# A matrix product by 11 block products instead of 12, with a new order of the steps around it

## The chip, the core and the metric

The kernel runs on one core of one Trainium2 chip. The metric is device time in microseconds: before, 270.99 us, the median of three runs (270.95 to 271.12). The core has a matrix engine (TensorE, PE in the profile, with PEld for its weight loads), three engines for elementwise work (VectorE or DVE, ScalarE or ACT, GpSimd or POOL) and SyncE (SP), which issues the transfers. Each takes its instructions strictly in the order in which the kernel writes them here.

## What is computed

Cross-attention with 8 heads of width 256, a residual and a layer norm. x is 16 batches x 256 rows x 256; the context has 16 batches x 77 rows x 192. All is float32.

```
Q = (x @ Wq)   K = (c @ Wk)   V = (c @ Wv)          # split into 8 heads of 256
score = Q K^T / sqrt(256), masked                   # 16 x 8 x 256 x 77
ctx = softmax(score) V, heads side by side          # 16 x 256 x 2048
out = ctx @ Wo + x
result = (out - mean) * rsqrt(var + eps) * gamma + beta
```

## The kernel before

**Folded weights.** Per head, Wq Wk^T / 16 is formed once (256 x 192: its transpose lies in `gA`, context columns 0 to 127, and in `gB`, columns 128 to 191, two heads in two halves of the partitions), and Wv Wo once (`uA`, `uB`). The context lies transposed in `cA` (128 partitions) and `cB` (64, in both halves). Per batch and head then A = g c^T (256 x 77) takes the place of Q and K, and scores are x A. `prepare_a` (line 168) makes A for a group of four batches and a pair of heads: `part_A` contracts 128 context columns in tiles of 128x32, `part_B` the other 64 in tiles of 64x32, 308 columns (4 x 77) at a time, into four banks. ACT copies these out (`copy_out`, line 960). `prepare_vw` (line 218) makes the same for values, one batch at a time, also in two parts.

**Softmax.** For each tile t of 128 rows (two a batch): `scores` (TensorE), `shift` (line 312: mask and row minimum, DVE, from two banks), `exponential` (ACT, eight heads, one instruction and one read of the sum each), `weigh` (reciprocal on DVE, two products on POOL), `turn` (transposition on DVE).

**Values.** `seven` (line 437) multiplies the weights of a batch's two tiles by seven instead of eight block products; it needs sums of the weights (`sums`, POOL, four instructions) and differences of the values (`differences`, POOL, one). `add_seven` (line 478) adds the products to x: two additions on DVE from PSUM, five on POOL. **Norm.** `finish` (line 500) makes mean and variance of a row tile (DVE), `spread` (line 522) the reciprocal deviation (ACT), `normalise` (line 565) two DVE instructions and the store.

**Order.** The main loop (line 977) runs b from -1 to 14. Step b works on three batches: scores and softmax of b + 1, `seven(b)`, norm of b - 1. Where (b + 1) is even, the step is long: `work_of(b + 1)` and `work_of(b + 2)` prepare the values of the next two batches and two pairs of heads of A for the next group. In a long step TensorE does scores, then parts A of the first work, parts B of both, parts A of the second, then `seven`; in a short step scores, then `seven`. What a short step leaves of its norm is done on DVE in the next step, after `shift` (`behind`). From b = 13 on, steps differ and stay as they are. All TensorE results go through eight PSUM banks in rotation (`ps_mm`): a new result waits until the one eight before it has been read.

**Setup.** Before the loop the weights are folded, A of the first group is made, the context's last part is turned (`turn_rest`, `turn_rest_last`, lines 634 to 641, with copies on POOL), and the last 13 context rows of all batches are multiplied (`prepare_last`, `pr`, eight banks, copied out by ACT and DVE in turn).

Of the kernel before, what the change touches and what calls it, by code (L numbers as in the profile page):

```python
# [27 lines left out]
def kernel(  # L28
# [52 lines left out]
    gB = const.tile([P, NF, DI], F32, tag="gB", name="gB")  # L81

# [85 lines left out]
    def prepare_a(g, places, lo=0, hi=GB, rest_first=False):  # L168


        if 0 in places:
            a_of[g] = in_two("a", [P, 2, GB, H, S2], g)
        parts = [
            (2 * u + i, dc) for u in places for dc in range(2) for i in range(2)
        ]
        batches = slice(g * GB + lo, g * GB + hi)
        each = GB // (hi - lo)
        whole = [
            ps_mm.tile([P, each, hi - lo, S2], F32, tag="mm", name=f"pa_{g}_{h}_{dc}_{lo}")
            for h, dc in parts[: len(parts) // each]  # L180
        ]
        banks = [w[:, i] for i in range(each) for w in whole]
        opening, closing = range(len(whole)), range(len(parts) - len(whole), len(parts))

        def cols(dc, i):
            return slice((2 * i + dc) * BK, (2 * i + dc + 1) * BK)

        wide = 2 if len(places) == 1 and g == 0 else 1

        def part_A():  # L190
            for n, ((h, dc), o) in enumerate(zip(parts, banks)):
                for i in range(NM):
                    nc.tensor.matmul(  # L193
                        flat(o[i * BK : (i + 1) * BK]),
                        gA[:, h, cols(dc, i)],
                        flat(cA[:, batches, :]),
                        start=not rest_first and n in opening,
                        stop=rest_first and n in closing,
                    )

        def part_B():
            for j in range(0, len(parts), 2):
                for i in range(0, NM, wide):
                    for k, (h, dc) in enumerate(parts[j : j + 2]):
                        nc.tensor.matmul(  # L205
                            flat(banks[j + k][i * BK : (i + wide) * BK]),
                            gB[half(k), h // 2, dc * P + i * BK : dc * P + (i + wide) * BK],
                            flat(cB[half(k), batches, :]),
                            start=rest_first and j + k in opening,
                            stop=not rest_first and j + k in closing,  # L210
                        )

        def copies():
            return [(a_of[g][:, dc, lo:hi, h, :], o) for (h, dc), o in zip(parts, banks)]

        return part_A, part_B, copies

# [94 lines left out]
    def shift(t):  # L312
# [17 lines left out]
        s_of[t] = s, top  # L330

# [168 lines left out]
    def finish(t):  # L500
# [3 lines left out]
        y = x_of(t)[:, 0, :]  # L504
        bn = st.tile([P, 6], F32, tag="bn", name=f"bn_{t}")
        nc.vector.bn_stats(bn, y)
        if j == 0:
            mv_of[g] = st.tile([P, GT, 2], F32, tag="mv", name=f"mv_{g}", bufs=2)
# [13 lines left out]
    def spread(first, last):  # L522
# [4 lines left out]
        nc.scalar.activation(log[:, lo:hi], mv_of[g][:, lo:hi, 1], AF.Ln, bias=eps)  # L527
# [72 lines left out]
    with tc.tile_pool(name="wonce", bufs=1) as wp:  # L600
# [33 lines left out]
        def turn_rest():  # L634
            nc.vector.transpose(flat(cA)[:, rest], flat(cA)[:, rest])
            nc.gpsimd.tensor_copy(cRA, cA[:, :, KM:])

        def turn_rest_last():
            nc.vector.transpose(flat(cB)[LB:, rest], flat(cB)[LB:, rest])
            nc.gpsimd.tensor_copy(flat(cB)[:LB, rest], flat(cB)[LB:, rest])  # L640
            nc.gpsimd.tensor_copy(cRB, cB[:, :, KM:])
# [163 lines left out]
        def g_of(e):  # L805
# [6 lines left out]
            nc.scalar.mul(gA[:, e], pg, D ** -0.5)  # L812
# [15 lines left out]
        def g_of_pair(a):  # L828
# [12 lines left out]
            for e, o in enumerate(banks):  # L841
                nc.scalar.mul(gA[:, 2 * a + e], o, D ** -0.5)
# [42 lines left out]
        for a in range(1, NF):  # L885
# [7 lines left out]
            a_of_pairs(a, rest_first=True)  # L893
        load_x(0)
# [10 lines left out]
        for j in range(NF // 2):  # L905
# [13 lines left out]
            for e, pw in enumerate(  # L919
# [3 lines left out]
                for i in range(2):  # L923
                    for k in range(2):
# [3 lines left out]
                        )  # L928
        for t in range(QT):
# [4 lines left out]
        turn_rest_last()  # L934
        sum_of(uB)
        for t in range(QT):
            exponential(t)
            weigh(t)

# [10 lines left out]
    def work_of(b, rest_first=False):  # L950
        g, n = b // GB + 1, b % GB
        work = [prepare_vw(b, rest_first)]
        if g < NG - 1 or g == NG - 1 and n < NF // 2:
            work.append(prepare_a(g, (n,), rest_first=rest_first))
        elif b <= NS:
# [21 lines left out]
    for b in range(-1, B - 1):  # L977
# [3 lines left out]
        for t in new if b >= 0 else ():  # L981
            scores(t)
        for t in new if b >= 0 else ():
# [8 lines left out]
        for m in range(0, 2) if b < 0 else range(b + 2, min(b + 3, B // 2)):  # L992
            turn_last(m)
        alone = b + 1 >= B - GB // 2
        works = work_of(b + 1) if alone or n % 2 == 0 else []
        for part_A, _, _ in works:
# [21 lines left out]
        for i, t in enumerate(new if b >= 0 else ()):  # L1018
            exponential(t)
            if old:  # L1020
                finish(old[i])
            weigh(t)
        ahead = works and not alone
        if old and not ahead:
            spread(old[0], old[-1] + 1)
        if ahead:
            copy_out(works)
            if old:
                spread(old[0], old[-1] + 1)
# [3 lines left out]
            for part_A, _, _ in works:  # L1033
# [6 lines left out]
        if b < NS:  # L1040
            if now:
                seven(b)
            if old:
                invert(old[0], old[-1] + 1)
                normalise(old[0])
            for t in new:
                turn(t)
            if b < 0:
                for t in range(QT, GT, 2):
                    transpose_x(t)  # L1050
                bias_of(GB, B)
# [8 lines left out]
            if now:  # L1060
                add_seven(b)
# [56 lines left out]
```

## Time and profile before

| what | us |
|---|---|
| median of the runs | 270.99 |
| the profiled execution, its own time | 269.95 |
| span of that execution | 268.2 |
| TensorE busy | 262.5 |
| DVE / ACT / POOL busy | 185.9 / 157.6 / 173.2 |

The span runs from the first to the last instruction of the profile; the rest of the 269.95 us lies around it. Busy times add up every instruction of an engine. The chain that ended last is followed back from the last instruction to whatever released each one; its lines give start, duration and what ran. In a timeline, a bracket at a line's end gives the idle time before it and the engine that ended it.

### The profile page before, as it was taken

The numbers are of one execution on the slowest core, as the hardware profiler recorded it, in microseconds if no ns is written. First come the engines' busy times: TensorE is split into PE (matmuls) and PEld (weight loads), VectorE is DVE, ScalarE is ACT, GpSimd is POOL, SyncE is SP. The second block draws the span as 40 slices with busy tenths as digits, with TensorE's granted clock in tenths as the row PEclk, the third lists the DMA queues.
The fourth block names the chain that finished last, engine by engine and source line by source line (L and its number), as shares of the span: only waits on it lengthen the run. The fifth ranks groups of instructions, "written<-read, shape, count | busy, mean of one in ns | idle before, by whom it ended". The sixth has DMA issues, their size and how long they took to land.

```text
span 268.2 us, 14455 instructions
## 1 busy us (share of the span) xinstructions
PE 262.5 (98%) x6090; PEld 191.8 (72%) x6090; DVE 185.9 (69%) x808; ACT 157.6 (59%) x667; POOL 173.2 (65%) x240
## 2 busy tenths in 40 slices
PE   8999999999999999999999999999999999999992
PEld 8566578944984699459944995499669957985662
DVE  1555967493583868665886379647977887799785
ACT  3243336536857565955596468737775595636772
POOL 1042005728399739994799669965998799585452
PEclk9999999999999999999999999999999999999999
DMA  6989987901500130232012401340034010100112
GB/s 190 217 199 228 334 138 142 311 21 34 129 7 2 46 80 2 63 111 71 5 43 90 112 5 43 91 113 2 6 120 122 4 45 2 44 22 22 46 40 80
DMA packets 41696, 22.69 MB, mean 85 GB/s; under 512 B 24144, under 2 KB 40608, under 8 KB 41632
## 3 DMA queue, kind: packets, MB, share of 16 engines
q1 hardware_dynamic: 41248, 20.98, 30.1%
q0 software_dynamic: 384, 0.79, 1.3%
q8 instruction: 48, 0.79, 1.3%
q14 instruction: 16, 0.13, 0.2%
HBM read 17.57 MB, written 4.19 MB: 81 GB/s over the span
## 4 chain that ended last, share of the span: by engine, by line
PE 98%; DVE 1%; issue 0%; DVEq 0%
PE ps L303 25%; PE pa L193 13%; PE pv L227 11%; PE po L450 11%; PE pm L450 8%; PE pa L205 6%; PE pv L238 6%; PE po L383 4%; PE pu L773 3%; PE pr L263 2%; PE pgb L834 2%; PE pw L787 1%; PE idle L703 1%; PE pr L274 1%; PE phb L850 1%; PE po L399 1%
## 5 line engine op out<-in xcount | busy, mean ns | idle before, releaser
L340 ACT ACTIVATE s<-s,top 128x77 f32<-128x77 f32 x256 | 85.3, 346 | 44.2 <-DVE top L320 37.9
L303 PE MATMUL ps<-a,xT 128*32 128x154 f32 x2048 | 69.9, 294 | 0.0
L303 PEld LDWEIGHTS ps<-a,xT 128*32 128x32 f32 x2048 | 66.2, 110 | 1.2 <-issue 0.4
L361 POOL TENSOR_TENSOR p<-s,rden 128x512 f32<-128x512 f32 x64 | 47.5, 768 | 29.5 <-DVE rden L355 29.4
L320 DVE CUSTOM_DVE_ANT_0 s<-ps,bias 128x77 f32<-128x77 f32 x256 | 43.5, 232 | 14.3 <-PE ps L303 14.3
L340 ACT ACTIVATION_READ_ACCUMULATOR s<-s,top 128x1 f32 x224 | 42.0, 187 | 0.0
L193 PE MATMUL pa<-cA,gA 128*32 128x308 f32 (+1 forms) x576 | 36.6, 395 | 0.0
L193 PEld LDWEIGHTS pa<-cA,gA 128*32 128x32 f32 x576 | 18.3, 110 | 21.0 <-issue 7.0
L484 POOL TENSOR_TENSOR xg<-xg,m 128x256 f32<-128x256 f32 x39 | 28.7, 736 | 6.6 <-DVE xg L498 4.5
L577 DVE SCALAR_TENSOR_TENSOR xg<-xg,rstd,bet 128x256 f32<-128x256 f32 x27 | 22.9, 847 | 14.0 <-ACT rstd L528 12.6
L227 PE MATMUL pv<-uA,cA 128*32 128x512 f32 x256 | 30.6, 595 | 0.0
L371 DVE STREAM_TRANSPOSE pT<-p 128x640 f32<-128x640 f32 x32 | 25.5, 821 | 3.4 <-POOL p L361 3.3
L414 POOL TENSOR_TENSOR ts<-vw 128x768 f32<-128x768 f32 x13 | 24.0, 1848 | 5.9 <-ACT vw L963 5.9
L963 ACT COPY vw<-pv 128x512 f32<-128x512 f32 x32 | 17.8, 584 | 14.8 <-PE pv L227 8.3
L498 DVE TENSOR_TENSOR xg<-po,xg 128x256 f32<-128x256 f32 x31 | 11.5, 405 | 13.8 <-PE po L450 13.3
L320 DVE DVE_READ_ACCUMULATOR2_ANT top<- 128x1 f32 x256 | 20.8, 81 | 0.0
L205 PE MATMUL pa<-cB,gB 64*32 64x308 f32 (+2 forms) x512 | 20.4, 387 | 0.0
L963 ACT COPY a<-pa 128x308 f32<-128x308 f32 (+1 forms) x56 | 18.9, 395 | 1.9 <-PE pa L193 0.4
L205 PEld LDWEIGHTS pa<-cB,gB 64*32 64x32 f32 (+1 forms) x512 | 11.0, 110 | 11.4 <-issue 6.2
L548 DVE SCALAR_TENSOR_TENSOR xg<-xg,mv,gam 128x256 f32<-128x256 f32 x30 | 17.6, 588 | 0.1
L238 PE MATMUL pv<-uB,cB 64*32 64x512 f32 x256 | 17.3, 597 | 0.0
L227 PEld LDWEIGHTS pv<-uA,cA 128*32 128x32 f32 x256 | 7.5, 109 | 12.8 <-issue 9.9
(119 smaller groups left out, 404.1 us busy)
## 6 DMA issues: line engine op xcount, KB each, us to landing
xg<-in_x_dram SPq DMA_DIRECT2D x8, 512.0 KB, 4.4
xT<-in_x_dram SPq DMA_DIRECT2D x56, 64.0 KB, 2.6
out_dram<-xg SPq DMA_DIRECT2D x11, 256.0 KB, 2.2
wo<-in_L_xattn_Wo_dram SPq DMA_DIRECT2D x4, 512.0 KB, 7.8
wq_blk<-in_L_xattn_Wq_dram SPq DMA_DIRECT2D x12, 128.0 KB, 4.3
out_dram<-xg SPq DMA_DIRECT2D x10, 128.0 KB, 1.9
wk_blk<-in_L_xattn_Wk_dram SPq DMA_DIRECT2D x12, 96.0 KB, 3.6
wvT<-in_L_xattn_Wv_dram POOLq DMA_DIRECT2D x8, 96.0 KB, 6.6
```

What stands on the lines that cost most here:

```text
L193: nc.tensor.matmul(flat(o[i * BK : (i + 1) * BK]), gA[:, h, cols(dc, i)], flat(cA[:, batches, :]), start=not rest_first and n in opening, ...
L205: nc.tensor.matmul(flat(banks[j + k][i * BK : (i + wide) * BK]), gB[half(k), h // 2, dc * P + i * BK : dc * P + (i + wide) * BK], flat(cB[ ...
L227: nc.tensor.matmul(pv[k][i * BK : (i + 1) * BK], cA[:, b, k * BK : (k + 1) * BK], uA[:, parts, :, i], start=not rest_first, stop=rest_first,)
L238: nc.tensor.matmul(pv[k][i * BK : (i + 1) * BK], cB[half(k), b, k * BK : (k + 1) * BK], uB[half(k), parts, :, i], start=rest_first, stop=n ...
L303: nc.tensor.matmul(ps[m // 2][i * BK : (i + 1) * BK, m % 2 * 2 * S2 : (m % 2 + 1) * 2 * S2], xT_of[t // PT][:, j * NM + m, dc], flat(a_of[ ...
L320: nc.vector.tensor_tensor_reduce(s[:, h], ps[a][:, k * S2 : (k + 1) * S2], bias[:, b, :], scale=-1.0, scalar=FAR, op0=ALU.add, op1=ALU.min ...
L340: nc.scalar.activation(s[:, h], s[:, h], AF.Exp, bias=top[:, one], scale=-1.0, accum_out=den[:, one] if summed_by_act(t) else None,)
L361: nc.gpsimd.tensor_tensor(part, e_mh[:, :, :, keys], rden_mh.unsqueeze(3).to_broadcast(list(part.shape)), ALU.mult,)
L371: nc.vector.transpose(pT_of[t].rearrange("p n m q -> p m n q"), p.rearrange("p m (n k) -> p m n k", k=BK),)
L450: nc.tensor.matmul(out[i * BK : (i + 1) * BK], weight[:, i], moving, start=first and n == 0, stop=final and n == len(terms) - 1,)
L484: nc.gpsimd.tensor_tensor(to, to, what, ALU.add)
L963: nc.scalar.copy(dst, src)
```

## The change

1. Ten of the pairs of heads (groups 1 and 2, and the first two pairs of group 3) are made by `prepare_fast` instead of `prepare_a`. The 256 x 192 matrix of a head is cut into blocks of 64 context columns by 128 rows, the context into the first two and the last two batches of a group (154 columns each). That would be 12 block products; by sums and differences of blocks made beforehand (`gS`, `gC` of the weights, `cT`, `cD` of the context) it is 11, each in tiles of 64x64. One product a head is needed in two sums: ACT copies it out alone, its bank slice is used again, and four DVE additions (`put_together`) make A from two banks and that copy.
2. Steps b = -1 to 8 become `quick_step`: both value products' 128-row parts, then `seven`, then all 64-row work; `finish` after both exponentials; `turn`, `sums`, `add_seven`, then the differences, the norm and, last in a long step, `put_together`. From b = 9 on the loop keeps its old form.
3. For batches 0 to 9 `finish` makes mean and variance on ACT, by two activations with a running sum.
4. Copies of `turn_rest` and `turn_rest_last` go from POOL to ACT. `gA` is stored with its columns in another order.

```diff
+    def sums_of_g():
+        for parts, sums, e, own, other in parts_of_g():
+            nc.scalar.copy(sums[own, 0, e], parts[other, 1, e])
+            nc.scalar.copy(gC[own], gB[other, :, P:])
+        for parts, sums, e, own, other in parts_of_g():
+            s1, s2, s3 = (sums[own, n, e] for n in range(3))
+            add(s1, s1, parts[own, 1, e])
+            subtract(s2, s1, parts[own, 0, e])
+            subtract(s3, parts[own, 0, e], parts[own, 1, e])
...
+    def sums_of_c(lo, hi):
+        xs, ys = halves_of(cA, lo, hi)
+        t1, t2, t3, t4 = (cT[:, n, lo - 1 : hi - 1] for n in range(4))
+        subtract(t1, ys, xs)
+        for own, other in ((low, high), (high, low)):
+            nc.gpsimd.tensor_copy(t2[own], ys[other])
+        subtract(t3, t2, ys)
+        subtract(t2, t2, t1)
...
+    def prepare_fast(g, u):
...
+        def middle(e):
+            h, own = heads[e], (high, low)[e]
+            return [
+                ((mids[e], 2), from_g(own, h, 0), c_of(cA, own, xs)),
+                ((mids[e], 0), from_s(own, 0, h), t_of(own, 0)),
+                ((mids[e], 2), from_s(own, 1, h), t_of(own, 1)),
+                ((mids[e], 1), from_s(own, 2, h), t_of(own, 2)),
+                ((mids[e], 1), lambda i: gC[own, u, half(i)], c_of(cB, own, ys)),
+            ]
+        def outer(e):
...
+        def pairs():
+            o, m = outer(0), middle(1)
+            ones = o[:2] + m[:1] + o[2:] + m[1:]
+            o, m = outer(1), middle(0)
+            return list(zip(ones, m[:1] + o[:3] + m[1:] + o[3:]))
+        def products():
...
+                for i in range(2):
+                    for ((bank, n), weight, moving), (start, stop, _) in zip(pair, flags):
+                        nc.tensor.matmul(bank[half(i), n], weight(i), moving, start=start, stop=stop)
+                for ((bank, n), _, _), (_, _, one) in zip(pair, flags):
+                    if one:
+                        nc.scalar.copy(blocks[lone[id(bank)]][:, 0], by_batch(bank)[:, n])
+        def plus(out, *of):
+            nc.vector.tensor_tensor(out, *of, ALU.add)
+        def put_together(e):
+            mid, end, of = by_batch(mids[e]), by_batch(ends[e]), blocks[e]
+            plus(of[:, 3], mid[:, 2], of[:, 0])
+            plus(of[:, 1:3], mid[:, 0:2], of[:, 3:4].to_broadcast([P, 2, HB, S2]))
+            plus(of[:, 3], mid[:, 0], of[:, 2])
+            plus(of[:, 0:3], end, of[:, 0:3])
+        return products, put_together
...
+    def by_act(t):
+        return fast(t // QT)
+    def fast(b):
+        return b < B - GB - GB // 2
...
+        if by_act(t):
+            junk = st.tile([P, DI], F32, tag="junk", name=f"junk_{t}", bufs=1)
+            mean, var = (mv_of[g][:, j, n : n + 1] for n in range(2))
+            nc.scalar.activation(junk, y, AF.Identity, scale=1.0 / DI, accum_out=mean)
+            nc.scalar.activation(junk, y, AF.Square, bias=mean, scale=-1.0, accum_out=var)
+            return
...
-            nc.gpsimd.tensor_copy(flat(cB)[:LB, rest], flat(cB)[LB:, rest])
-            nc.gpsimd.tensor_copy(cRB, cB[:, :, KM:])
+            nc.scalar.copy(flat(cB)[:LB, rest], flat(cB)[LB:, rest])
+            nc.scalar.copy(cRB, cB[:, :, KM:])
...
+    def quick_step(b):
...
+        if b >= 0:
+            for t in new:
+                exponential(t)
+                weigh(t)
+        for t in old:
+            finish(t)
+        if old:
+            spread(old[0], old[-1] + 1)
+        fasts = []
+        if long:
+            works = work_of(b + 1) + work_of(b + 2)
+            for part_A, *_ in works:
+                part_A()
+        if now:
+            seven(b)
+        if long:
+            for _, part_B, _ in works:
+                part_B()
+            for k in range(2):
+                fasts.append(prepare_fast(g, n + k))
+                if k == 0:
+                    copy_out(works[:1])
+                fasts[k][0]()
+                if k == 0:
+                    copy_out(works[1:])
+        for t in new:
+            turn(t)
...
+        sums(b + 1)
+        if now:
+            add_seven(b)
+        if long:
+            for k in range(2):
+                differences(b + 1 + k)
...
+        if long:
+            if old:
+                normalise(old[0])
+            turn_x_and_normalise(g, n, old)
+            for _, put_together in fasts:
+                put_together(0)
+                put_together(1)
+        else:
+            if old:
+                behind.append(partial(normalise, old[0]))
+            behind.append(partial(turn_x_and_normalise, g, n, old))
+
+    ready = B - GB - GB // 2 - 1
+    for b in range(-1, ready):
+        quick_step(b)
+    for b in range(ready, B - 1):
```

More of the change, by code (lines that the diff above doesn't have):

```diff
@@ L893 @@
             a_of_pairs(a, rest_first=True)
+        gS = const.tile([P, 3, H, P], F32, tag="gS", name="gS")
+        sums_of_g()
         load_x(0)
@@ L952, in work_of @@
         work = [prepare_vw(b, rest_first)]
[L953 to L955 removed]
+        if b <= NS and not fast(b):
             part = (0, 2) if g < NG else (2, GB)
@@ L980 @@
         new = range((b + 1) * QT, (b + 2) * QT)
-        for t in new if b >= 0 else ():
+        g, n = (b + 1) // GB + 1, (b + 1) % GB
+        long = n % 2 == 0
+        if b >= 0:
+            for t in new:
+                scores(t)
+            for t in new:
+                shift(t)
+        while behind:
+            behind.pop(0)()
+        if long and g < NG:
+            load_x((g * GB + n) // 2)
+        for m in range(0, 2) if b < 0 else range(b + 2, min(b + 3, B // 2)):
+            turn_last(m)
@@ L991 @@
             load_x((g * GB + n) // 2)
-        for m in range(0, 2) if b < 0 else range(b + 2, min(b + 3, B // 2)):
-            turn_last(m)
         alone = b + 1 >= B - GB // 2
-        works = work_of(b + 1) if alone or n % 2 == 0 else []
-        for part_A, _, _ in works:
+        ahead = not alone and n % 2 == 0
+        works = work_of(b + 1) if alone or ahead else []
+        for part_A, *_ in works:
             part_A()
@@ L1017 @@
             break
-        for i, t in enumerate(new if b >= 0 else ()):
+        for i, t in enumerate(new):
             exponential(t)
-            if old:
-                finish(old[i])
+            finish(old[i])
             weigh(t)
-        ahead = works and not alone
-        if old and not ahead:
-            spread(old[0], old[-1] + 1)
         if ahead:
             copy_out(works)
-            if old:
-                spread(old[0], old[-1] + 1)
+        spread(old[0], old[-1] + 1)
+        if ahead:
             works = work_of(b + 2, rest_first=True)
@@ L1032 @@
                 part_B()
-            for part_A, _, _ in works:
+            for part_A, *_ in works:
                 part_A()
@@ L1040 @@
         if b < NS:
[L1041 to L1045, printed above, removed]
+            seven(b)
+            invert(old[0], old[-1] + 1)
+            normalise(old[0])
             for t in new:
                 turn(t)
[L1048 to L1051, printed above, removed]
             if alone or ahead:
```

125 lines of the change are left out of this document (114 added, 11 removed).

## The prediction

> **What bounds the kernel now.** I read the share of the chain that ended last first, then that chain in order of time, then the busy times of one period, then the queues of VectorE (DVE), ScalarE (ACT) and GpSimd (POOL) in order of time.
>
> ```profile
> PE 98%; DVE 1%; issue 0%; DVEq 0%
> ```
>
> ```profile
> 134.95 1.72 PE pv L227 x16
> 136.67 2.07 PE pa L193 x32
> 138.74 1.02 PE pv L238 x16
> 139.76 1.04 PE pa L205 x32
> 140.79 0.86 PE pv L238 x16
> ...
> 142.69 1.85 PE pv L227 x16
> ...
> 146.62 1.75 PE pm L450 x64
> ...
> 150.54 4.19 PE ps L303 x128
> ...
> 162.83 1.72 PE pv L227 x16
> ```
>
> ```profile
> 134.77:162.65 27.88, 27.88 (x713) 20.22 (x705) 19.10 (x96) 18.18 (x83) 22.53 (x31) 1.00 0.21 60
> ```
>
> The chain is TensorE nearly from end to end. Its pieces touch: two steps (one "long", with the preparation of two batches, one "short") take 162.83 - 134.95 = 27.88 us, without a gap and at a granted clock of 1.00. The preparation, 134.95 to 146.62, is 11.67 of it; scores and seven products are the other 16.21, 8.1 a step, of which scores are 4.19. In the same window DVE works 19.10 us, ACT 18.18, POOL 22.53 (the columns after PE and PEld). So only TensorE's queue counts now, and a gain there lasts until another engine's queue is as long. Busy sums don't tell when that is: an engine in order also waits. So I lay out the waits.
>
> **TensorE's gain.** One pair of heads costs 2.07 + 1.04 = 3.11 us now (L193 and L205). Afterwards it is 11 products x 2 heads x 2 column halves = 44 matmuls of 154 columns, four at a time in 64x64 tiles. The profile shows every matmul as two instructions, so 88, or 22 fours. The scores, also 154 columns, run 128 instructions in 4.19 us: 0.131 us a four, so 2.88 us. For the 64x64 form there are these rows (start, duration):
>
> ```profile
> 13.29 1.10 PE L850 MATMUL phb<-qT,kT_all 64*64 64x128 f32 x32
> 14.22 1.91 PE L834 MATMUL pgb<-qT,kT_all 64*64 64x256 f32 x32
> ```
>
> 32 instructions of 128 columns take 14.22 - 13.29 = 0.93 us, 0.116 a four; scaled to 154 columns that is 0.140, or 3.08 us. So a pair gains 0.03 to 0.23 us; I take 0.23, since the scores have the right width. `prepare_fast` runs in the long steps b = -1, 1, 3, 5, 7, twice each: 10 x 0.23 = 2.3 us. Putting the 64-row work in one block removes no change of tile shape: there is one entry to 64 rows now (1.02 against 0.86 for the same work, 0.16 us) and one return (1.85 against 1.72, 0.13). A change from 64x32 to 64x64 tiles is added; before has none. I bound it by 0 and 0.16 and take 0.1, 0.5 us in five steps. TensorE alone would then need 27.88 - 2 x 0.23 + 0.1 = 27.5 us a period and save 1.8 us in all. The Trainium skill, "TensorEngine Tiling (Array Packing)", Tiling Modes, Key Properties, says that changing the tiling mode, not just the tile, drains the engine; by it the added change costs like the other entry, 0.8 us in five steps, and the 0.16 above agrees.
>
> **What VectorE gets for it.** Before, ACT copied the four A banks out. Now ACT copies one slice a head, and `put_together` is four DVE additions a head: 154, 308, 154 and 462 columns, one operand in PSUM. The trace has the same operation at two sizes:
>
> ```profile
> L498 DVE TENSOR_TENSOR xg<-po,xg 128x256 f32<-128x256 f32 x31 | 11.5, 405 | 13.8 <-PE po L450 13.3
> ```
>
> ```profile
> L516 DVE TENSOR_TENSOR xg<-po,xg 128x128 f32<-128x128 f32 x2 | 0.6, 286 | 0.0
> ```
>
> The slope is (405 - 286)/128 = 0.93 ns a column, so 0.31, 0.45, 0.31 and 0.60 us. The first three each feed the next, and a dependent instruction starts 0.04 after the end of the one before (145.88 + 0.44 to 146.36, below); independent ones overlap by some 0.1 (two of 0.83 in 1.56, below). One head: 1.6 us (1.3 if all overlap, 1.8 if none does). A long step has four heads: **6.4 us** (5.2 to 7.2). It stands at the end of the long step, and the next step's `shift` is queued behind it on DVE. Taken off DVE are the row statistics, but these fill waits of DVE for ACT today, so I count nothing for them.
>
> So DVE's queue closes a loop over two steps. Its short leg, from the first `shift` instruction to the end of the product additions, is in these rows:
>
> ```profile
> 151.65 0.24 DVE L320 CUSTOM_DVE_ANT_0 s<-ps,bias 128x77 f32<-128x77 f32 x1 [0.29 <-PE ps L303]
> 157.62 0.20 DVE L355 RECIPROCAL rden<-den 128x8 f32<-128x8 f32 x1 [0.96 <-ACT s L340]
> 159.29 1.56 DVE L371 STREAM_TRANSPOSE pT<-p 128x640 f32<-128x640 f32 x2
> 160.77 0.71 DVE L498 TENSOR_TENSOR xg<-po,xg 128x256 f32<-128x256 f32 x2
> ```
>
> ```profile
> 157.90 1.69 POOL L361 TENSOR_TENSOR p<-s,rden 128x512 f32<-128x512 f32 x2 [0.29 <-DVE rden L355]
> ```
>
> The second tile's reciprocal comes 5.97 us after the first `shift`, with ACT's 16 exponentials in between without a pause. POOL's weighing ends at 159.59, the second tile's transposition takes half of 1.56, the additions 0.71: 7.94 + 0.78 + 0.71 = **9.4 us**, which no order in the diff shortens. Only then, on DVE's queue, can the long step's `shift` run:
>
> ```profile
> 133.55 0.22 DVE L320 CUSTOM_DVE_ANT_0 s<-ps,bias 128x77 f32<-128x77 f32 x1
> 136.08 0.57 DVE L548 SCALAR_TENSOR_TENSOR xg<-xg,mv,gam 128x256 f32<-128x256 f32 x1
> 137.45 0.70 DVE L293 STREAM_TRANSPOSE vr<-vr 128x512 f32<-128x512 f32 x1
> 144.69 1.26 DVE L165 STREAM_TRANSPOSE xT<-xT 128x512 f32<-128x512 f32 x2
> 145.88 0.44 DVE L548 SCALAR_TENSOR_TENSOR xg<-xg,mv,gam 128x256 f32<-128x256 f32 x1
> 146.36 0.84 DVE L577 SCALAR_TENSOR_TENSOR xg<-xg,rstd,bet 128x256 f32<-128x256 f32 x1
> ```
>
> ```profile
> 140.62 2.90 POOL L361 TENSOR_TENSOR p<-s,rden 128x512 f32<-128x512 f32 x4
> ```
>
> `shift` 2.53 (133.55 to 136.08); two normalisations left over from the short step, 1.35 each (136.08 to 137.45, 145.88 to 147.20); one `vr` transposition 0.63; two reciprocals 0.2; POOL's weighing 2.90; the second transposition 0.78; additions 0.71; a normalisation, two `xT` transpositions and a normalisation 1.35 + 2.51. Together 14.3 us, then 6.4 of `put_together`: 20.7. **The loop is 9.4 + 20.7 = 30.1 us**, against 27.5 for TensorE after the change and 27.88 before. In today's order the same sum without `put_together` is 23.7, and TensorE hides it. Now it is DVE that sets the pace, and TensorE's 0.4 us a period is gone. Where the lateness reaches it: the first part of the sum that `prepare_fast` makes for a head stands in a bank slice that is used again, so the sixth pair of products waits for ACT's copy of it after the first, five pairs of 0.26 us later; ahead of that copy stand on ACT the exponentials, whose `shift` was late, `finish`, `spread`, the copy of `m` and those of `pv`, which also free banks of the same products. Excess 30.1 - 27.88 = 2.2 us, four periods (b = 1 to 9): 8.8. DVE enters the first of them early, being idle in b = -1; I take off half a period's excess: **+7.7** (a loop of 28.9 or 30.9 by the bounds of `put_together`, reckoned the same way: +3.6 to +10.6).
>
> The Trainium skill, "GPSIMD Engine Reference", Specifications, says that POOL shares its SBUF interface with VectorE and that instructions with two SBUF inputs contend. L577, with two, shows 0.84 above; L498, with one operand in PSUM, took 0.71 for two while POOL was busy. If the page's rule reached PSUM operands too, and stretched the additions by, say, a half, the loop would grow by 3.2 us; the trace is against that.
>
> **The start.** The copies of `turn_rest_last` move from POOL to ACT, ahead of the exponentials of the first batch, which on ACT stand ahead of the copies of `pr`:
>
> ```profile
> 48.79 0.93 POOL L640 COPY cB<-cB 64x896 f32<-64x896 f32 x1 [3.49 <-DVE cB L639]
> 49.78 0.36 POOL L641 COPY cRB<-cB 128x208 f32<-128x208 f32 x1
> ```
>
> ```profile
> 54.06 1.80 ACT L133 COPY vr<-pr 128x416 f32<-128x416 f32 x4 [3.28 <-PE pr L274]
> ```
>
> At the same prices ACT is through both at about 50.1, and with 16 exponentials (5.5 us, as in the 5.97 above) at 55.6. The copies of `pr`, which free the banks of the first `pv`, begin 1.5 us later than 54.06, and TensorE with them; the smaller preparation of b = -1 gives 0.4 back: **+1.1 us** (0.5 to 1.6). ACT's copies for `sums_of_g` and POOL's sums lie in idle time before 40 us; the sums of C before step b = -1 leave POOL enough time until the products need them. No DMA is added; the two loads of `xT` go out together, later on SP, and are turned a long step later.
>
> **The handover at b = 9.** The first step of the old form has exponential, `finish`, exponential, `finish` on ACT, as `by_act` still holds for batches 8 and 9. `finish` waits for batch 8's last addition on POOL, and `quick_step(8)` puts `sums(9)` ahead of it. Between these rows POOL does just this work, additions and sums, without a pause:
>
> ```profile
> 133.87 0.99 POOL L484 TENSOR_TENSOR m<-m 128x128 f32<-128x128 f32 x2
> 137.20 0.92 POOL L431 TENSOR_TENSOR ss<-pT 128x256 f32<-128x256 f32 x1
> ```
>
> From 133.87 to 140.62 it is 6.75 us. The price of ACT's statistics isn't shown; the nearest rows:
>
> ```profile
> L561 ACT ACTIVATE xg<-xg,rstd 128x256 f32<-128x256 f32 x3 | 1.5, 510 | 0.3 <-DVE xg L548 0.2
> ```
>
> ```profile
> L340 ACT ACTIVATION_READ_ACCUMULATOR s<-s,top 128x1 f32 x224 | 42.0, 187 | 0.0
> ```
>
> Two activations and two reads: 1.4 us end to end, 1.0 with no read; I take 1.1. Let T be the end of the last transposition of step 8. The sum is complete at T + 6.75; then `finish` 1.1, eight exponentials 2.7, `finish` 1.1, two copies 1.1: the banks of `pv` come free at T + 12.8. In the steady loop T lies 9.4 - 0.7 = 8.7 after the short step's first `shift`, that 3.2 to 4.6 after its scores begin (half to three quarters of `put_together`), and the scores of b = 9 begin 8.1 after those: T is 3.8 to 5.2 after them. TensorE needs the banks here:
>
> ```profile
> 186.53 4.19 PE ps L303 x128
> ...
> 195.91 0.52 PE pa L205 x32
> ```
>
> 195.91 - 186.53 = 9.4 us after these scores begin, and gets them at 16.6 to 18.0: a stall of **8 us** (4.4 if the additions should be done when the first exponentials end).
>
> **Rivals.** (1) **TensorE keeps the pace, faster.** It needs the loop at most 27.5, 2.6 less than my sum: `put_together` at 3.8 instead of 6.4. With no hole at b = 9 either, 1.8 us are saved: 269.95 - 1.8 + 1.0 (to the median, below) = 269.2, faster, if the start is hidden too; with the start's 1.5 it is 270.7, no change. For it: every busy sum stays below the period. Against it: 3.8 us is less than the columns alone (1,078 x 4 x 0.93 ns = 4.0). (2) **The loop only**: `finish` doesn't hold ACT at b = 9; 269.95 + 1.1 + 7.7 + 1.0 = 279.8. (3) **The handover only**: loop about 27.9; 269.95 + 1.1 + 8 + 1.0 = 280. (4) The 64x64 products don't run four at a time: not below 3.11 a pair, no gain, and the same loop; it changes my time by nothing, since TensorE waits anyway.
>
> **How the numbers follow.** The profiled execution took 269.95 us for a span of 268.2; the median of the runs is 270.99, 1.0 more, which I add. Forecast 269.95 + 1.1 + 7.7 + 8 = 286.8, with 1.0 **287.8**. Low end: start 0.5, loop 3.6, handover 4.4, 279.5; rivals 2 and 3 at some 280; a little below them 277. High end: 1.6 + 10.6 + 8.6 and 2 us of lag left in the steps after b = 9: 293.8; I take 295. Chances: forecast 0.60, rivals 2 and 3 0.12 each, rival 1 0.16, of which 0.04 with the start's cost, which is no change; rival 4 sits inside the forecast. About 0.2% is what a measurement of this kernel can tell from no change. Faster 0.12, same 0.04, slower 0.84.
>
> **What would show it.** Right: period of two steps near 30 us between b = 3 and b = 9, TensorE idle at the `pf` products or scores with ACT or DVE as releaser, `shift` following directly on the last addition of `put_together`, a hole of several us on TensorE at `pa` L205 in b = 9. Wrong: a chain still 98% TensorE and a period of 27.5; additions shorter than 0.2 us.

## The result, and the profile after

| | before | after |
|---|---|---|
| median, us (lowest to highest) | 270.97 (270.86 to 271.12, 4 runs) | 286.16 (285.49 to 286.43, 4 runs) |
| profiled execution, us (span) | 269.95 (268.2) | 285.92 (283.8) |
| first scores of b = 1, us | 74.81 | 76.44 |
| first scores of b = 9, us | 186.34 | 196.82 |
| first scores of b = 10, us | 203.08 | 217.71 |

The kernel after is slower: ratio 1.0557, 95% interval 1.0536 to 1.0577. The forecast was 287.8.

The page of the kernel after: span, busy times, two of the rows of slices (busy share of TensorE and its granted clock, each digit the tenths of a fortieth of the span), and the shares of the chain that ended last.

```profile
span 283.8 us, 15133 instructions
PE 265.9 (94%) x6330; PEld 205.1 (72%) x6330; DVE 205.3 (72%) x848; ACT 172.7 (61%) x736; POOL 188.7 (66%) x262
...
PE   8999999899998999979998999799968999999992
...
PEclk9999999999999999979999999999999999999999
...
DVE 25%; POOL 16%; ACT 13%; PE 9%; issue 3%; DVEq 0%; POOLq 0%; ACTq 0%
```

TensorE's row on the page of the kernel before:

```profile
PE   8999999999999999999999999999999999999992
```

The chain that was 98% TensorE now goes round through DVE, POOL and ACT, TensorE's row has holes in the middle where it had none, and the granted clock one dip (a 7). No engine but TensorE, which now waits, is near full: DVE has 72%. Busy shares would not have told this; a queue of instructions in order, with its waits, is the bound.

The same by periods of two steps, from the scores of b = 1 to those of b = 9. The first number after the window is its length, then PE, PEld, DVE, ACT and POOL busy, and the granted clock.

```profile
76.44:105.64 29.20, 28.29 (x761) 22.87 (x757) 21.29 (x99) 17.06 (x81) 21.30 (x29) 1.00 0.19 45
105.64:137.79 32.15, 30.16 (x761) 24.40 (x755) 24.92 (x106) 22.06 (x105) 22.82 (x31) 0.95 0.23 59
137.79:166.58 28.79, 27.82 (x760) 22.64 (x756) 23.59 (x102) 18.67 (x85) 20.69 (x28) 1.00 0.17 51
166.58:196.82 30.24, 28.49 (x760) 22.72 (x756) 23.35 (x102) 20.36 (x95) 21.73 (x29) 1.00 0.21 56
```

Together 120.38 us, 30.1 a period, where before had 4 x 27.88 = 111.5. Now DVE in order of time over one period: `shift` of the long step, its norm and transpositions, the additions, `shift` of the short step.

```profile
142.27 0.22 DVE L485 CUSTOM_DVE_ANT_0 s<-ps,bias 128x77 f32<-128x77 f32 x1
...
148.44 0.22 DVE L526 RECIPROCAL rden<-den 128x8 f32<-128x8 f32 x2
150.08 0.84 DVE L542 STREAM_TRANSPOSE pT<-p 128x640 f32<-128x640 f32 x1 [1.43 <-POOL p L532]
151.42 0.84 DVE L542 STREAM_TRANSPOSE pT<-p 128x640 f32<-128x640 f32 x1 [0.49 <-POOL p L532]
152.19 0.72 DVE L669 TENSOR_TENSOR xg<-po,xg 128x256 f32<-128x256 f32 x2
...
156.49 7.28 DVE L372 TENSOR_TENSOR a<-pf,a 128x154 f32<-128x154 f32 x16
163.68 0.23 DVE L485 CUSTOM_DVE_ANT_0 s<-ps,bias 128x77 f32<-128x77 f32 x1
...
166.90 0.20 DVE L526 RECIPROCAL rden<-den 128x8 f32<-128x8 f32 x1 [0.61 <-ACT s L511]
169.63 0.20 DVE L526 RECIPROCAL rden<-den 128x8 f32<-128x8 f32 x1 [2.53 <-ACT s L511]
...
172.74 0.22 DVE L485 CUSTOM_DVE_ANT_0 s<-ps,bias 128x77 f32<-128x77 f32 x1
```

The 16 additions (L372) take 7.28 us, and the next step's `shift` (L485) starts at 163.68 directly on their end. From 142.27 to 163.68 the long leg is 21.4 us; the short leg, to 172.74, is 9.1. ACT stood idle for the whole length of the additions:

```profile
164.01 0.36 ACT L511 ACTIVATE s<-s,top 128x77 f32<-128x77 f32 x1 [7.26 <-DVE top L485]
```

Where TensorE paid for it, by its own waits (total, times, longest):

```profile
PE pm L621 <- ACT vw L1145: 3.4, 1, 3.4
PE pf L360 <- DVE xg L669: 3.1, 4, 1.0
PE pf L360 <- ACT m L646: 1.9, 3, 0.7
PE pv L392 <- ACT vr L142: 1.2, 1, 1.2
PE pv L392 <- ACT m L646: 0.6, 2, 0.3
```

The first row is b = 9 alone, the fourth is the start, the others are the loop. They add up to less than the loss, in part because the clock fell behind the longest of the loop's waits (last section), which took 1.7 us of TensorE's time; the rest isn't traced.

The 16.0 us between the two profiled executions divide, by the scores' starts in the table, into 1.6 at the start (76.44 - 74.81), 8.9 in the four periods (120.38 - 111.53) and 4.1 in the step b = 9 (20.89 us against 16.74); 1.3 is behind it, 0.4 of that outside the span.

### The profile page after: what moved, and what is told of

The parts are those of the page before. It is cut to its first block, busy times and chain, and to the rows that moved or that the text cites. A ratio compares the mean times of both kernels' runs of the same rounds, so it can differ in the third digit from the quotient of the medians.

```text
span 283.8 us, 15133 instructions
## 1 busy us (share of the span) xinstructions
PE 265.9 (94%) x6330; PEld 205.1 (72%) x6330; DVE 205.3 (72%) x848; ACT 172.7 (61%) x736; POOL 188.7 (66%) x262
## 4 chain that ended last, share of the span: by engine, by line
DVE 25%; POOL 16%; ACT 13%; PE 9%; issue 3%; DVEq 0%; POOLq 0%; ACTq 0%
ACT s L511 11%; POOL p L532 7%; PE pf L360 6%; DVE pT L542 5%; DVE s L485 4%; DVE a L372 4%; PE ps L468 4%; DVE xg L725 3%; POOL xg L655 3%; DVE xg L754 3%; DVE xg L669 2%; POOL ss L603 1%; POOL ss L604 1%; POOL ss L602 1%; POOL ss L605 1%
## 5 line engine op out<-in xcount | busy, mean ns | idle before, releaser
L532 POOL TENSOR_TENSOR p<-s,rden 128x512 f32<-128x512 f32 x64 | 45.2, 730 | 40.3 <-DVE rden L526 40.2
L485 DVE CUSTOM_DVE_ANT_0 s<-ps,bias 128x77 f32<-128x77 f32 x256 | 41.6, 230 | 0.0
L372 DVE TENSOR_TENSOR a<-pf,a 128x154 f32<-128x154 f32 x80 | 33.6, 436 | 2.8
L655 POOL TENSOR_TENSOR xg<-xg,m 128x256 f32<-128x256 f32 x39 | 29.7, 763 | 2.7 <-DVE xg L669 0.7
L526 DVE RECIPROCAL rden<-den 128x8 f32<-128x8 f32 x32 | 6.0, 193 | 32.0 <-ACT s L511 31.8
L754 DVE SCALAR_TENSOR_TENSOR xg<-xg,rstd,bet 128x256 f32<-128x256 f32 x27 | 18.7, 692 | 6.9 <-ACT rstd L705 5.2
L485 DVE DVE_READ_ACCUMULATOR2_ANT top<- 128x1 f32 x256 | 20.5, 80 | 0.0
L360 PE MATMUL pf<-cT,gS 64*64 64x154 f32 x240 | 18.8, 306 | 0.0
L360 PEld LDWEIGHTS pf<-cT,gS 64*64 64x64 f32 x240 | 17.0, 141 | 0.0
L602 POOL TENSOR_TENSOR ss<-pT 128x256 f32<-128x256 f32 x13 | 9.7, 745 | 10.7 <-DVE pT L542 10.7
L360 PE MATMUL pf<-cA,gA 64*64 64x154 f32 x160 | 11.6, 302 | 5.0 <-DVE xg L669 3.1
```

The source lines that it names most:

```text
L360: nc.tensor.matmul(bank[half(i), n], weight(i), moving, start=start, stop=stop,)
L372: nc.vector.tensor_tensor(out, *of, ALU.add)
L485: nc.vector.tensor_tensor_reduce(s[:, h], ps[a][:, k * S2 : (k + 1) * S2], bias[:, b, :], scale=-1.0, scalar=FAR, op0=ALU.add, op1=ALU.min ...
L532: nc.gpsimd.tensor_tensor(part, e_mh[:, :, :, keys], rden_mh.unsqueeze(3).to_broadcast(list(part.shape)), ALU.mult,)
L655: nc.gpsimd.tensor_tensor(to, to, what, ALU.add)
L754: nc.vector.scalar_tensor_tensor(y, y, rstd, bet, ALU.mult, ALU.add)
```

## Experiments

Theory: **DVE's loop** (short leg, long leg with the additions at its end) sets the period; the wait of b = 9 and the start are separate terms. Rivals: the new order or the 64x64 products themselves are slow, or the pace is set by ACT with its statistics. The ratio is to the kernel before, run on the same chip (270.1 to 270.4 us there).

| run | edit | us | ratio, 95% |
|---|---|---|---|
| e1 | additions of two heads behind the next `shift` | 282.00 | 1.0420 to 1.0451 |
| e2 | statistics on ACT for batches 0 to 7 only | 281.74 | 1.0400 to 1.0440 |
| e3 | new order, 12 products as before | 274.40 | 1.0141 to 1.0172 |
| e4 | statistics all on DVE | 282.28 | 1.0430 to 1.0476 |
| e5 | additions and norms into DVE's waits, e2's edit | 273.24 | 1.0089 to 1.0123 |
| e6 | the start's copies back on POOL | 285.62 | 1.0545 to 1.0594 |
| e7 | e5 and e6 | 274.46 | 1.0131 to 1.0178 |
| e8 | e5, but one head's additions put off | 273.04 | 1.0074 to 1.0107 |
| e9 | e8, start's copies on POOL, sums of C placed | 270.65 | 1.0001 to 1.0019 |
| e10 | e9, one POOL addition later | 270.78 | 1.0009 to 1.0030 |
| e11 | e9, one normalisation later | 270.03 | 0.9977 to 1.0001 |
| e12 | e11, sums of C spread | 269.74 | 0.9958 to 0.9986 |

**e3: which half of the change costs?** The 11 products and `put_together` are replaced by `prepare_a`, in the new order.

```diff
-                fasts.append(prepare_fast(g, n + k))
+                plain = prepare_a(g, (n + k,), rest_first=True)
...
-                fasts[k][0]()
+                plain[1]()
+                plain[0]()
...
-            for _, put_together in fasts:
-                put_together(0)
-                put_together(1)
```

> The quick steps keep their order, their statistics on ACT and all sums made beforehand, but A comes from the twelve products of before (parts B, then A, four banks, ACT copies them out) in the place of the eleven, so the 16 additions of a long step are gone from DVE. Theory (the additions make the loop too long): loop 30.3 - 7.2 = 23, TensorE paces at 27.9 a period as before; left are the start (1.6) and the hole at b = 9, at most 4: 272 to 276 us. Rival (the new order of the steps itself is what costs): 282 us or more.

274.40. Two of its periods:

```profile
96.80:124.98 28.18, 28.18 (x708) 20.02 (x704) 17.91 (x88) 22.77 (x99) 21.09 (x30) 1.00 0.21 60
124.98:153.16 28.18, 28.18 (x708) 20.02 (x704) 17.90 (x88) 22.77 (x99) 21.83 (x30) 1.00 0.22 60
```

TensorE is busy for the whole of each. ACT's 22.8 us of work don't slow it, and b = 9 has no hole (17.03 us against 16.74 before). The period is 0.3 us over before. That fits the tile shapes: here TensorE goes to 64-row tiles and back twice a period, once for each pair of heads, before only once, and there the change cost 0.16 us and the one back 0.13. So 286.16 - 274.40 = 11.8 us come with the 11 products and their additions: the loop and, through its lateness, the handover (20.89 us).

**e1: is it the place of the additions on DVE?**

```diff
-            for _, put_together in fasts:
-                put_together(0)
-                put_together(1)
+            for e in range(2):
+                fasts[0][1](e)
+            behind.extend(partial(fasts[1][1], e) for e in range(2))
```

> The additions of the second pair of heads (8 of the 16 of a long step) go behind the shift of the next step; nothing else is changed. Theory (DVE's in-order queue closes a loop of 30.3 us over two steps): 3.6 us leave the long leg and fall in the short step, where DVE waits 0.6 + 2.5 us for ACT's exponentials anyway, so the loop becomes about 27.5 and TensorE paces again: four periods x 2.8 = 11 us less, 275 us. Rival (TensorE waits for banks that the additions of products and the copy of m free, and the place of the additions doesn't matter): 286 us, within 1 us.

282.00, between the two. The direction was the loop's, the size not. DVE in the short step of e1:

```profile
158.54 0.23 DVE L485 CUSTOM_DVE_ANT_0 s<-ps,bias 128x77 f32<-128x77 f32 x1
...
162.01 3.61 DVE L372 TENSOR_TENSOR a<-pf,a 128x154 f32<-128x154 f32 x8
165.54 0.26 DVE L526 RECIPROCAL rden<-den 128x8 f32<-128x8 f32 x2
167.22 0.84 DVE L542 STREAM_TRANSPOSE pT<-p 128x640 f32<-128x640 f32 x1 [1.43 <-POOL p L532]
```

The eight additions stand in front of both reciprocals. In the kernel after, the first of them comes 3.2 us after the first `shift` (166.90 - 163.68); here both come after 7.0, so POOL weighs both tiles one after the other with DVE waiting (1.43). The short leg grew from 9.1 to 11.4 and gave back two thirds of the 3.6 won in the long one; period 29.2. Moving work behind the urgent instruction isn't enough: it must fit into a wait.

**e2 and e4: what do the statistics on ACT cost?** `by_act(t)` returns `t // QT < 8` in e2 and `t // QT < 0` in e4, so that in b = 9 `finish` no longer stands between ACT's exponentials, and in e4 no statistics are on ACT at all.

> Row statistics on ACT only for batches 0 to 7; those of batches 8 and 9 on DVE, as the steps b = 9 and 10 had them before. Theory (at b = 9 ACT stands between two exponentials, waiting for POOL's last addition of batch 8): the idle of 3.4 us on TensorE ahead of the seven products of b = 9 goes, 282.5 us. Rival (the idle is only the lag of DVE's loop arriving at the first step of the old form): 286 us.

> Row statistics on DVE for all batches, eleven products and order as in the changed kernel. Theory (on DVE they fall mostly into its waits for ACT and POOL, so moving them to ACT bought little; the hole at b = 9 goes): loop longer by at most 0.5 us, 4 x 0.5 - 3.5: 283 to 285 us. Rival (DVE's busy time is what counts: 4 x 0.5 us more of it in each period): 286 + 8 - 3.5 = 290 us or more.

281.74 and 282.28. In both, the row "PE pm <- ACT vw" is gone from TensorE's waits: 4.4 us in e2, about what the step b = 9 had lost. With the statistics back on DVE the period from b = 3 on is 30.6 (DVE's loop 30.6 against 30.5), hardly longer: they fill DVE's waits, as the prediction counted them. ACT doesn't set the pace.

**e5: the additions in DVE's waits.** The second pair's heads go behind the first and the second reciprocal of the next step, of the two normalisations that a short step leaves over, one stays ahead of the first reciprocal of the long step and the other goes behind it; e2's edit is in it too.

```diff
+        fill = behind[:]
+        behind.clear()
...
+            if long:
+                fill.pop(0)()
+            weigh(new[0])
+            if fill:
+                fill.pop(0)()
...
+            weigh(new[1])
...
-            for _, put_together in fasts:
-                put_together(0)
-                put_together(1)
+            for e in range(2):
+                fasts[0][1](e)
+            behind.extend(partial(fasts[1][1], e) for e in range(2))
```

> Second pair's additions in the next step, but behind the first tile's reciprocal (first head) and the second tile's (second head); in long steps one leftover normalisation stays ahead of the first tile's reciprocal and the other goes behind it; statistics on ACT for batches 0 to 7 only. No work is added or left out. Theory (DVE's queue with its waits sets the period): short leg 9.1 + 1.0, long leg 21.4 - 3.6 - 1.4, loop 26.5, so TensorE paces at 27.5 to 28: 286.2 - 4 x 2.5 - 4.4 = 271.5 us, 270.5 to 273. Rival (DVE's sum of work, not its waits, is what is too long): as with the additions merely put later and the statistics as in the second run, 277 to 278 us.

273.24: 8.5 below e2. Periods of 27.59 and 28.9 alternate; where a group changes, the scores want A of the last head before its additions are done:

```profile
105.45 1.78 PE L468 MATMUL ps<-a,xT 128*32 128x154 f32 x48 [0.93 <-DVE a L372]
```

**e6 and e7: the start.** The copies of `turn_rest_last` go back to POOL, and the sums of C for later groups behind the step b = -1; e7 is this on e5.

> Only the start: the copies of the context's last part back on POOL, POOL's sums of C behind the first weighing, those for groups 2 and 3 after the first differences. Theory (ACT's copies delay the first exponentials and so the copies of pr): TensorE's 1.15 us of idle ahead of the first values go, 285 us; DVE's loop then carries on from 1 us earlier. Rival (DVE's 7.3 us of additions in step -1 set when the loop begins, and they don't move): 286.2 us.

> The two above together. Theory: the shares add, 270.4 us (269.5 to 272), about as before the change or a little faster. Rival (a new wait takes the place of the one removed): 273 us or more.

e6 is inconclusive: 285.62, an interval that overlaps that of the kernel after. The wait at `pv` is gone and the scores of b = 1 start at 74.41 instead of 76.44; 0.8 of these 2.0 us is there at the first scores of all (41.74 against 42.55), ahead of everything that the edit moves. The loop behind takes 0.8 back until b = 9 (195.62 against 196.82), and the step b = 9 takes 22.59 us instead of 20.89: there TensorE's clock was at half for 3.4 us, which it was not in the kernel after (last section). e7 shows the start gain too (75.19) and missed its forecast by 4: POOL's sums of C for two groups (72.10 to 77.34) stood in front of a weighing, and the period from b = 1 took 30.0.

**e8 and e9: only the last head put off, and the sums of C placed.** In e8 the list of the long step is

```diff
+            for f, e in ((0, 0), (0, 1), (1, 0)):
+                fasts[f][1](e)
+            behind.append(partial(fasts[1][1], 1))
```

and e9 adds e6's copies, with one group's `sums_of_c` at the end of b = 1 and of b = 3.

> As e5_filled, but of the second pair only the last head's additions are put off, to behind the next short step's first reciprocal; the other three heads' stay at the end of the long step. Loop theory: VectorE's loop is then a short leg of about 9.1 us (the additions of one head, 1.8, fill the wait between the two reciprocals and lengthen nothing) and a long leg of 21.4 - 1.8 - 1.4 (one normalisation moved into the wait for the first reciprocal) = 18.2, together 27.3, just under TensorE's 27.5 to 27.6. The scores at b=3 and b=7 no longer wait for A, which cost 1.35 us each in e5_filled. Periods of 27.6 all through, first scores of b=9 at about 187; time about 271.8 (270.8 to 272.8) against 270.4 to 271 before: what is left over is the start. Rival (the place of the additions hardly matters, a new wait for banks or for GpSimd takes the place of the old one): 273 or more, as e5_filled.

> As e8_last_head, and the two copies of turn_rest_last back on GpSimd as in e6_start_pool, the sums of C for later groups made at the end of b=1 and b=3 instead of before or in b=-1, so that GpSimd's weighing of the first steps isn't behind them (what held up e7_filled_start). Theory: scores of b=1 at about 75 instead of 76.5, periods of 27.6, first scores of b=9 at about 185.5; time about 270.2 (269.5 to 271), within half a per cent of before on either side. Rival (the second start fix is eaten by the loop, or the sums of C on GpSimd hold up a weighing elsewhere): 271.5 or more, no better than e8_last_head.

e8 missed (273.04), though the scores no longer wait; e9 came near (270.65, 0.1% over before). Two of e9's periods, and POOL in the long step between:

```profile
102.51:130.10 27.59, 27.59 (x761) 22.66 (x756) 23.45 (x104) 19.84 (x91) 23.93 (x37) 1.00 0.23 60
130.10:158.45 28.35, 27.82 (x761) 22.62 (x756) 24.21 (x105) 20.36 (x95) 22.54 (x31) 1.00 0.26 71
```

```profile
137.91 2.67 POOL L655 TENSOR_TENSOR xg<-xg,m 128x256 f32<-128x256 f32 x3
140.54 2.71 POOL L532 TENSOR_TENSOR p<-s,rden 128x512 f32<-128x512 f32 x4
```

DVE's loop was 28.5, not the 27.3 of my sum: the normalisation that I moved into the wait for the first reciprocal saved 0.2 instead of 1.4, since POOL, held by the additions of the step before, didn't weigh ahead of 140.54, 2.2 after that reciprocal. DVE waited for POOL in place of ACT.

**e10: POOL's last addition behind the weighing,** and in the long step both transpositions of `xT` ahead of both normalisations.

> As e9_last_head_start, but GpSimd's last addition of a short step's seven products (the third on x, for the second row tile only) is put behind the next long step's weighing, and there the two transpositions of xT go ahead of both normalisations. In e9 the two later periods took 28.35 and 28.46 us against TensorE's 27.59: in the long step GpSimd is held by sums and additions until 140.54, the weighing ends at 143.2 and the second transposition waits for it, although the second reciprocal was ready at 140.7 and one tile's weighing is 1.35. Theory (the loop through VectorE and GpSimd still sets these two periods): 0.9 us less in each of them, so that TensorE sets all four at 27.6; first scores of b=9 about 1.6 us earlier, near 185.3; time about 269.1 (268.5 to 269.8), faster than before's 270.4 by some 0.5%. Rival (the excess lies elsewhere, or the later statistics of the second tile on ScalarE hold up the normalisation by as much): 270.4 to 270.9, as e9.

It came out as the rival has it, 270.78. DVE's loop got shorter only to 28.1, and ACT paid:

```profile
142.56 0.42 ACT L684 ACTIVATE junk<-xg 128x256 f32<-128x256 f32 x1 [1.96 <-POOL xg L655]
```

ACT's statistics wait for the addition, with the copies of `m`, `pv` and the first sums queued behind.

**e11 and e12: a normalisation into the short step's two waits; then the sums of C of the last group spread over POOL's waits.** e11's edit:

```diff
+            if held:
+                centre(held[0])
...
+            if held and t == new[1]:
+                normalise(held.pop(), centred=True)
             turn(t)
...
-            turn_x_and_normalise(g, n, old)
+            turn_x_and_normalise(g, n, ())
+            held.extend(old[1:])
```

> As e9_last_head_start (GpSimd's order untouched), but the long step's second normalisation (1.35 us on VectorE, ahead of the additions) is put off into the next short step: its first instruction behind the additions that fill the wait between the two reciprocals, its second into the 0.78 us in which VectorE waits for GpSimd between the two transpositions. Theory (the two later periods of e9, 28.35 and 28.46, are VectorE's loop, and in the long step the time ahead of the additions counts in full): loop 28.45 - 1.35 + 0 to 0.45 = 27.1 to 27.55, so that TensorE sets all four periods at 27.6 and its 0.5 us wait at the pf products goes; first scores of b=9 near 185.4 instead of 186.9; time about 269.2 (268.6 to 269.8), 0.3 to 0.6% faster than before. Rival (the additions wait for TensorE's products anyway, or the short leg grows by as much): 270.4 or more, as e9 and e10.

> As e11_last_tile, but the eight instructions that make the sums of C for the last group on GpSimd no longer stand at the end of b=3 (where they end at about 129.7, 2 us after the reciprocal for which the next weighing is due): three go between the weighings of b=4, two to the end of b=5, three between the weighings of b=6, where GpSimd waits 1.1 to 1.4 us. Theory (the one slow period left in e11, 28.02 us from b=5 to b=7, follows from that late weighing): all four periods at 27.6, first scores of b=9 at 185.4; time about 269.6 (269.2 to 270.0), 0.1 to 0.3% faster than before. Rival (the slow period has another cause): 28 us stays, 270.0 or more.

e11: 270.03, the loop as expected and three of four periods at TensorE's 27.6; its interval still holds 1, so no gain is shown. e12 was ahead of before: 269.74 against 270.30 on the same chip, ratio 0.9972 (0.9958 to 0.9986), 0.3%. That is little: the single runs of the two kernels overlap (268.86 to 270.61 against 269.83 to 271.03). Its four periods:

```profile
75.31:102.89 27.58, 27.58 (x760) 22.64 (x755) 21.16 (x98) 17.96 (x86) 24.32 (x37) 1.00 0.16 40
102.89:130.56 27.67, 27.67 (x760) 22.63 (x756) 24.41 (x105) 20.19 (x94) 22.53 (x33) 1.00 0.26 70
130.56:158.25 27.69, 27.69 (x761) 22.63 (x757) 24.15 (x104) 20.56 (x96) 23.64 (x35) 1.00 0.21 56
158.25:185.83 27.58, 27.58 (x760) 22.65 (x755) 23.33 (x102) 20.64 (x97) 22.09 (x30) 1.00 0.26 68
```

TensorE is busy for the whole of every window. This is what the 11 products are worth against before when nothing stands in their way: some 0.25 us a period of 27.88. Against 12 products in the same order (e3, 28.18) it is 0.55, of which e3's second change of tile shape and back would be 0.3.

## Why the prediction was right

**The bound.** It is DVE's loop, as forecast, with the `shift` on the heels of the last addition, ACT idle for the length of the additions, and the chain off TensorE. e3 without the additions has TensorE's pace, and e5 to e12 with the same additions in DVE's waits come back to it or near it, in some periods at first and in e12 in all four.

**TensorE's gain.** A pair of products takes 2.9 us after (forecast 2.88), the least period 27.58 (forecast 27.5). The difference fits the higher of the two bounds for the added change of tile shape, 0.16 rather than the 0.1 that I took. That the 64x64 form doesn't run four at a time is out.

**The loop: mechanism right, term mis-sized.** Forecast 30.1 us and +7.7; measured 30.4 on DVE and +8.9 on TensorE. The term that was off is `put_together`: taken at 6.4, it measured 7.28 from its first start to its last end and 7.19 to the start of the next `shift`, at my upper bound of 7.2. Three things make the difference. My own terms add up to more than I wrote: 1.67 for a head's four additions, three times 0.04 for those that feed the next and 0.1 off for an overlap are 1.69, not 1.6, so 6.8 a long step. The additions are longer than the slope gave, 1.75 a head instead of 1.67, so 0.3 more:

```profile
L372 DVE TENSOR_TENSOR a<-pf,a 128x462 f32<-128x462 f32 x4 | 2.6, 640 | 0.3
L372 DVE TENSOR_TENSOR a<-pf,a 128x154 f32<-128x154 f32 x8 | 2.5, 313 | 0.1
L372 DVE TENSOR_TENSOR a<-pf,a 128x308 f32<-128x308 f32 x4 | 1.9, 479 | 0.1
```

And ahead of the four longest DVE stood still for 0.3 us in all (first row) instead of 0.16. How they follow each other was as I took it. Within a head the next starts 0.03 after the end of the one before; between heads, where nothing is passed on, it starts 0.08 ahead of the end, as `shift` does behind the last (163.68 against 156.49 + 7.28):

```profile
157.34 0.32 DVE L372 TENSOR_TENSOR a<-pf,a 128x154 f32<-128x154 f32 x1
157.70 0.64 DVE L372 TENSOR_TENSOR a<-pf,a 128x462 f32<-128x462 f32 x1
158.25 0.31 DVE L372 TENSOR_TENSOR a<-pf,a 128x154 f32<-128x154 f32 x1
```

Against the longer term the long leg ahead of the additions was 14.2 instead of 14.3, the short one 9.1 instead of 9.4. The Trainium skill, "VectorE: DVE Perf Modes", The DRAIN you can't avoid, has the pipe empty after each instruction before the next starts, and lets one that is not held start earlier; these rows show both.

**Where TensorE feels it: the place was wrong.** I let the sixth pair of products wait for ACT's copy of the first sum. The waits stand at the products' first use of a bank, and are for ACT's copy of `m` and DVE's additions from `po` (rows above), which free banks of the same step. Strictly taken in turn, as I had described the eight banks, these products would have found others; so the order in which banks are given out isn't the one I assumed. The kernel's pace is DVE's either way, so the size didn't suffer.

**The handover: right in kind, twice too large.** Forecast 8 us (4.4 as low end), measured 4.1. (In its sum, three quarters of `put_together` are 4.8 us, not 4.6, which moves one end by 0.2.) ACT and TensorE in b = 9:

```profile
208.33 0.42 ACT L681 ACTIVATE junk<-xg 128x256 f32<-128x256 f32 x1 [2.17 <-POOL xg L655]
...
213.15 1.05 ACT L1145 COPY vw<-pv 128x512 f32<-128x512 f32 x2
```

```profile
213.76 0.64 PE L621 MATMUL pm<-vw,pT 128*32 128x128 f32 x16 [3.45 <-ACT vw L1145]
```

`finish` does hold ACT's exponentials for POOL's sum, and the copies of `pv` come late. But the hole stands at `pm`, not at the products ahead of it: TensorE did the second work's products first (its last row ahead of the hole ends at 210.31), which I had put behind a stall at 9.4 us after the scores, 206.2, for want of banks. So 4.1 us of its work lay beside ACT's lateness. This is the same wrong assumption on the banks, and here it cost 4 us of the forecast. e2 removes the hole and 4.4 us with it.

**The start.** Forecast 1.1, measured 1.6. 0.7 is there already at the first scores (42.55 against 41.85). Its cause isn't shown; with the same kernel up to there the runs here have them between 41.74 and 42.64, so it may be scatter. 1.15 is TensorE's wait for ACT's copy of `pr`, the one that was forecast. e6 removes it.

**The sum** was 286.8 for the profiled execution; it took 285.92. Against the forecast the loop is 1.2 longer, the handover 3.9 shorter, the start 0.5 longer, and 1.3 at the end wasn't forecast: 0.9 less in all. That it came so near is errors of both signs; the mechanisms are what held.

## What to carry to other kernels

When work is taken off a full engine and given to one that is 70% busy, lay out the second engine's instructions in order, with its waits, over one turn of the loop: what is queued in front of the instruction that others wait for counts in full, what fits into a wait counts nothing; the additions and the handover that came late with them cost 11.8 us in one place (after against e3), and in the other (e12) the same additions leave TensorE without a wait in the loop. Before a wait is filled, look at the engine that ends it: where that is held by a queue of its own, filling moves the wait and saves little (e8, e10).

## What the runs showed of the hardware

**TensorE's clock was halved for 3.4 us behind some idle stretches and not behind others, and a loop elsewhere can hide that.** The long second period (32.15 us) holds two holes of 0.67 and 1.00 us, followed by a lower granted clock:

```profile
120.00:124.00 4.00, 2.33 (x48) 1.78 (x44) 3.41 (x7) 3.03 (x10) 2.90 (x5) 0.91 0.50 131
123.28:126.69 3.41, 3.41 (x64) 3.41 (x59) 3.34 (x7) 1.10 (x3) 3.17 (x6) 0.50 0.17 58
124.00:128.00 4.00, 4.00 (x91) 4.00 (x87) 3.86 (x9) 0.96 (x3) 3.69 (x7) 0.66 0.02 4
128.00:132.00 4.00, 4.00 (x127) 3.77 (x120) 3.69 (x10) 0.00 (x0) 4.00 (x3) 1.00 0.02 4
```

At 0.66 TensorE gets through 91 instructions in 4 us, where 127 pass at 1.00. The fourth period has nearly as much idle time in 4 us, with the clock at 1.00 then and after. At b = 9 the kernel after and e6 have the same hole, 3.45 us ahead of `pm`; the clock stays in the first and falls in the second:

```profile
180.00:184.00 4.00, 2.54 (x53) 1.39 (x41) 3.08 (x6) 3.21 (x11) 2.98 (x5) 1.00 0.19 24
212.00:216.00 4.00, 2.24 (x76) 2.06 (x80) 1.14 (x3) 3.94 (x16) 3.23 (x3) 1.00 0.48 131
212.00:216.00 4.00, 3.41 (x76) 2.99 (x80) 1.76 (x3) 3.97 (x16) 2.71 (x4) 0.71 0.47 131
```

The first two rows are of the kernel after, the third is of e6. So the length of a hole alone doesn't decide; what does isn't shown here. What it costs depends on who sets the pace. The period behind the long one is shorter again (28.79), because DVE kept its own pace: the first exponentials behind the short steps' `shift` start at 103.08, 133.54, 164.01 and 194.25, 30.2 to 30.5 us apart, so in the loop the clock cost time that TensorE had to spare. In e6's step b = 9 the same 3.4 us at half clock stand beside 1.7 us more. The Trainium skill, "TensorE: Matmul & The Clock Gate", What's actually happening, lets the clock fall after at least one idle window of about 3.4 us; the rows show it lower after 1.67 us of idle time in 4, in two pieces, and at 1.00 after a hole of 3.45. Its section A second HAM failure mode has frequent short idle stretches between groups of matmuls lower the clock in another kernel; the second period agrees with that, the fourth doesn't.

**Additions of one operand in PSUM kept their price beside POOL.** POOL was busy for 3.69 and 4.00 of the 4 us in which DVE made most of those of the second period (124 to 132 above), and an addition took 436 ns on average, where the prediction's slope gave 1.67 / 4 = 418. The half more that a contention would have cost isn't there: the one of 462 columns that stands alone, behind POOL's last work of the step, takes as long as the one at 157.70 beside POOL.

```profile
159.14 3.62 POOL L585 TENSOR_TENSOR ts<-vw 128x768 f32<-128x768 f32 x2
163.13 0.64 DVE L372 TENSOR_TENSOR a<-pf,a 128x462 f32<-128x462 f32 x1
```
